# First batch of a scan, attention and expert kernel: x asked for first, u and the projected rows used where they lie, the first time steps two halves at a time, other stores put off

## The chip, the cores and the metric

The kernel runs on one core of a Trainium2 chip. The metric is the device time of one execution in microseconds (us). TensorE is PE in the profile (its weight loads are PEld), VectorE DVE, ScalarE ACT, GpSimd POOL and SyncE SP. SP issues nearly all DMAs of this kernel; its queue entries are SPq.

## What is computed

The input x is (4, 384, 32, 32), four batches of 384 channels on 32 x 32 pixels. Three parts follow each other in each batch; a group normalisation stands before the first.

- A selective scan over four directions (by rows, by columns, and both reversed). For each direction k: `x_dbl = u . x_proj[k]` gives 12 rows for the time step, 16 rows B and 16 rows C; `dt = softplus(dts . dt_proj + bias)`; then for each channel and each of the 16 states, along the 1024 pixels, `h = h * exp(dt * A) + dt * u * B` and `y = sum over the states of h * C`. The four directions' y and `D * u` are added, normalised over the channels, and put through a gelu.
- Windowed causal attention with six heads over 256 tokens, with a gated projection.
- A mixture of four experts, two for each token: 384 to 1536 to 384.

All of it is in f32.

## The kernel before, in words

**Tiles.** Channels lie on the 128 partitions in three tiles (T = 3), pixels along the free dimension (L = 1024, in NH = 2 halves of 512). For the scan a block is 32 channels with 4 states each on the 128 partitions, so a channel tile has 4 blocks (`j`) and a block has 4 groups of states (`g`). A slot is one block and one group, 128 x 1024; there are 16 turns (4 batches x 4 directions) of 48 slots, 768 slots.

**One slot.** `times_b` multiplies dt*u by the B rows into z on POOL, `decay` computes dA = exp(dt * A) on ACT into PSUM, `scan` runs the recurrence on DVE. The product with C follows on POOL (the scan's result then lies in z) or on DVE (it lies in dA), as the planner chooses. `fold_y` adds the 4 states of each channel on PE and adds the sum to what is in DRAM (`ydr`).

**How a slot is fed.** `state_rows` loads B and C rows from DRAM, repeated over 32 channels (`bc`, 512 KB each, 8 for a turn). `time_steps` computes dt and dt*u for one channel tile, in two halves: a matmul of the projected rows `xd` with `dtw` into PSUM (`ps_dt`), then softplus on ACT and DVE, in tiles `ed`; the results go to DRAM (`dtr`), from where `spread` loads them repeated over four states (`dts`).

**Before the first scan.** Constants are loaded on SP's queue; `a4`, the A of every slot, is made from A_logs by four matmuls and a few DVE steps. Then `group_norm(0)`: x is loaded (`xn`) for the moments on DVE, a chain of small matmuls gives mean and scale of each group (`g`), x has meanwhile been loaded again (`un`) and is normalised on ACT, stored as u in `udr`; D * u in two orders is made on ACT (`yd`) and stored to `ydr`. `project` loads u back (`ux`), multiplies it with the projection weights (`ps_x`), copies the result in row order and column order into `xo`, and stores it to `xdr`. `turn_loads` reads the 12 time-step rows back (`xd`) with their weights (`dtw_sb`), `time_steps` reads u once more (`ub`).

**What sets the order.** The whole program is written out ahead of time by a planner (`Machine`). Every generator asks for its next instruction; the planner holds a clock for each engine, costs for each operation, and due times, and picks what can start first, with a bias for EARLY work. So each engine has one fixed order, and another beginning gives another order everywhere. Buffers come from `Stock`s (`wts` of 8 weight tiles, `zs_` of 7 z tiles, `eds` of 3 tiles ed, `pts_` of 3 tiles pt, `banks` of 4 PSUM banks). The first turn's direction is 1, by columns.

The scan of later batches runs while attention and experts of earlier batches fill PE; after the last scan the attention of the last batch and what remains of the experts is left as a tail.

Of the kernel before, what the change touches and what calls it, by code (L numbers as in the profile page):

```python
# [11 lines left out]
F32 = mybir.dt.float32  # L12
# [378 lines left out]
def conv_attn_hybrid(  # L391
# [11 lines left out]
    def const_load(src, shape, name):  # L403
        dst = const.tile(shape, F32, name=name)
        nc.sync.dma_start(dst, src)
        return dst

    xw_sb = const_load(xw, [P, T, KG, XR], "xw_sb")
# [19 lines left out]
    nc.vector.tensor_reduce(dsum, ds_sb.rearrange("p k t -> p t k"), AX.X, ALU.add)  # L428

    fold = const.tile([P, 32], F32, name="fold")  # L430
    nc.vector.tensor_reduce(fold, ident.rearrange("p (d s) -> p d s", s=SG), AX.X, ALU.add)
# [38 lines left out]
    nc.vector.memset(ones, 1.0)  # L470
# [19 lines left out]
    with tc.tile_pool(name="setup", bufs=1) as setup:  # L490
        count_i = setup.tile([P, MB], mybir.dt.int32, name="count_i")
        nc.gpsimd.iota(count_i, pattern=[[1, MB]], base=0, channel_multiplier=0)
        nc.vector.tensor_copy(count, count_i)
        nc.vector.tensor_scalar(count_p, count[:, :SEG], float(P), None, ALU.mult)
        nc.vector.tensor_scalar(base_e, count[:, :NE], float(SEG), None, ALU.mult)
        al_sb = setup.tile([P, KG, T, NS], F32, name="al_sb")
        nc.sync.dma_start(al_sb, alog)
        sel = setup.tile([P, JB, P], F32, name="sel_j")
        nc.gpsimd.memset(sel, 1.0)
        nc.gpsimd.affine_select(  # L500
            sel.rearrange("p j (d s) -> p j d s", s=SG), sel.rearrange("p j (d s) -> p j d s", s=SG),
            pattern=[[-32, JB], [-1, 32], [0, SG]], compare_op=ALU.is_equal, fill=0.0,
            base=0, channel_multiplier=1,
        )
        own = setup.tile([P, SG], F32, name="own")
        nc.vector.tensor_reduce(own, ident.rearrange("p (d s) -> p s d", s=SG), AX.X, ALU.add)
        for j in range(JB):
            ps = banks.now("ps_al")
            pv = ps[:, : KG * T * NS]
            nc.tensor.matmul(  # L510
                pv, sel[:, j, :], al_sb.rearrange("p k t n -> p (k t n)"), start=True, stop=True
            )
            am = setup.tile([P, KG * T * NG, SG], F32, tag="am", name="am")
            nc.vector.tensor_tensor(
                am, pv.rearrange("p (f s) -> p f s", s=SG), bcast(own, KG * T * NG), ALU.mult
            )
            nc.vector.tensor_reduce(
                a4[:, :, :, j, :], am.rearrange("p (k t g) s -> p k t g s", k=KG, t=T), AX.X, ALU.add
            )
            banks.give(ps)  # L520
        m.load_exp_ln()
        m.table = "exp_ln"
        nc.scalar.activation(a4, a4, AF.Exp)
        nc.vector.tensor_scalar(a4, a4, -1.0, None, ALU.mult)

# [14 lines left out]
    pts_ = Stock(m, work, "pt", 3, [P, 4 * P])  # L540
# [4 lines left out]


# [39 lines left out]
    def on_vector():  # L586
        lead = FAVOUR if count_of["scan"] < NSLOT else 0.1
        return m.clock["dve"] + lead < m.clock["act"]

# [48 lines left out]

    def group_norm(b):
# [3 lines left out]
        us_ = us_all if b else zs_  # L643
        mv = rp.tile([P, T, 2], F32, tag="mv", name="mv", bufs=1)

        def moments(t):
            u = yield from us_.take("xn")
            yield from sp.dma_start(u, x[b, ts(t, P)].rearrange("p h w -> p (h w)"))
            st = yield from sts.take("st")
            for h in range(NH):  # L650
                yield from dve.bn_stats(st[:, 6 * h : 6 * h + 6], u[:, ts(h, HB)])
            yield from dve.bn_aggr(mv[:, t, :], st)
            us_.give(u)
            sts.give(st)
# [28 lines left out]
        def normal(t):  # L683
            u = yield from us_.take("un")
            yield from sp.dma_start(u, x[b, ts(t, P)].rearrange("p h w -> p (h w)"))
            yield from act.activation(
                u, u, AF.Identity, bias=g_off[:, t : t + 1], scale=g_rstd[:, t : t + 1]
            )
            yield from sp.dma_start(udr[b][t], u)
            yd = yield from zs_.take("yd")  # L690

# [4 lines left out]
            us_.give(u)  # L696
# [5 lines left out]
            zs_.give(yd)  # L702

        yield from m.together([normal(t) for t in range(T)], T if b == 0 else 1, EARLY)
        have.add(("u", b))


        def project(pair):
            xos = yield from zs_.take("xo", n=2)
            for h in range(NH):  # L710
                us = yield from us_.take("ux", n=2)
                uv = [us[t // NH][:, ts(t % NH, HB)] for t in range(T)]
                for t in range(T):
                    yield from sp.dma_start(uv[t], udr[b][t][:, ts(h, HB)])
# [9 lines left out]
                us_.give(*us)  # L724
                yield from act.copy(xos[0][: 2 * XR, ts(h, HB)], pv)
                yield from copy(
                    xos[1][: 2 * XR, :].rearrange("r (w h) -> r h w", h=HH)[:, ts(h, HH // NH), :],
                    pv.rearrange("r (h w) -> r h w", w=WW),
                )
                banks.give(ps)  # L730
            for n in (1, 0):
                yield from sp.dma_start(xdr[b][2 * pair + n], xos[n][n * XR : (n + 1) * XR, :])
                have.add(("x", b, 2 * pair + n))
            zs_.give(*xos)

        yield from m.together([project(pair) for pair in (0, 1)], 2 if b == 0 else 1, EARLY)

    def turn_loads():
        for i, (b, k) in enumerate(turns):
            yield lambda: ("x", b, k) in have and (i == 0 or (i - 1, T - 1) in dtrs)  # L740
# [7 lines left out]
            xds[i], dtws[i] = xd, dtw_sb  # L748
# [13 lines left out]
    def time_steps():  # L762

        for i, (b, k) in enumerate(turns):
            for t in range(T):
                yield lambda: i in xds and ("u", b) in have and count_of["scan"] >= (i * T + t) * TS - 40
                u = yield from us_all.take("ub")
                yield from sp.dma_start(u, udr[b][t])


                dtr = dram.tile([2, P, L], F32, tag="dtr", name="dtr", bufs=4)
                bias = dtb_sb[:, k, t : t + 1]
                for h in range(NH):
                    c, r = ts(h, HB), slice(32 * h, 32 * h + R)
                    e, dt = yield from eds.take("ed", n=2)
                    w = yield from banks.take("ps_dt", 0)
                    yield from pe.matmul(w, dtws[i][r, ts(t, P)], xds[i][r], start=True, stop=True)
                    yield from act.activation(e, w, AF.Abs, bias=bias)
                    yield from act.activation(dt, w, AF.Relu, bias=bias)
                    yield from act.activation(e, e, AF.Exp, scale=-1.0)  # L780
                    yield from act.activation(w, e, AF.Identity, bias=1.0)
                    yield from dve.scalar_tensor_tensor(e, w, -1.0, e, ALU.add, ALU.subtract)
                    yield from act.activation(w, w, AF.Ln)
                    yield from dve.tensor_tensor(w, w, e, ALU.subtract)
                    yield from dve.tensor_tensor(w, w, dt, ALU.add)
                    if k % 2:
                        v = slice(h * (WW // NH), (h + 1) * (WW // NH))
                        yield from dve.tensor_tensor(
# [807 lines left out]
```

## Time and profile before

| what | value |
|---|---|
| time, median of 4 runs | 3817.52 us (3815.51 to 3819.78) |
| profiled execution, its own time | 3820.98 us |
| its span | 3819.2 us |
| busy share: PE, DVE, ACT, POOL | 79%, 77%, 58%, 74% |
| mean granted clock of PE | 0.83 |
| first scan starts | 97.90 us |
| last scan ends | 3117.97 us |
| DMA over the span | 953.64 MB, 250 GB/s |

The span is the profiled time from the first to the last instruction. A share is a mean over stages with different limits, so what matters is when each engine is busy: the lines are shown with the prediction. In the order of time a row gives start, length, engine, operation, result and inputs, and in brackets the idle time of the engine before it with what ended it. Buffer numbers are left out of names. A helper records nearly all operations, so most have its lines, L148 or L159; rows are told apart by their tiles. A matmul in f32 leaves two records.

### The profile page before, as it was taken

What the parts mean: (1) busy time and instruction counts of PE and PEld (TensorE: products, weight loads), DVE (VectorE), ACT (ScalarE), POOL (GpSimd) and SP (SyncE); (2) the same over time, 40 slices, a digit from 0 to 9 for tenths busy, and PEclk for the clock granted to TensorE, in tenths of its full rate; (3) what the DMA queues carried; (4) which work ended last, traced back from release to release, by engine and by line L of the source; (5) the groups of instructions that cost most, each with busy time, mean ns of one, the idle gap of its engine ahead of it and who ended that gap; (6) DMA issues with size and microseconds to landing.
All of it is one profiled execution on the core that took longest, in us unless ns stands there. A gap on an engine that the chain in (4) does not pass through costs nothing. (4 is left out here: it accounts for less than half of the span.)

```text
span 3819.2 us, 50289 instructions
## 1 busy us (share of the span) xinstructions
PE 3006.0 (79%) x15892; PEld 1822.5 (48%) x15892; DVE 2932.8 (77%) x3341; ACT 2220.9 (58%) x4028; POOL 2810.7 (74%) x1469
## 2 busy tenths in 40 slices
PE   2555545578797899877678788898898999998998
PEld 1100010035564555544356445565555668777886
DVE  2999999998889999999988989988789963321001
ACT  2545545467676677776667576777767654442221
POOL 0999998999888887999988699898889960102001
PEclk8555556578798899986779899998898999998997
DMA  5776775444468899944478789675679974468995
GB/s 198 270 263 219 266 261 216 169 161 142 162 226 344 324 370 324 365 159 159 137 251 281 281 321 345 241 252 179 219 266 362 348 258 149 159 212 306 318 318 189
DMA packets 394144, 953.64 MB, mean 250 GB/s; under 512 B 49620, under 2 KB 173400, under 8 KB 393880
## 3 DMA queue, kind: packets, MB, share of 16 engines
q1 hardware_dynamic: 385688, 925.27, 68.5%
q0 software_dynamic: 8192, 25.17, 1.9%
q8 instruction: 126, 2.06, 0.2%
q14 instruction: 138, 1.13, 0.1%
HBM read 786.39 MB, written 182.78 MB: 254 GB/s over the span
## 5 line engine op out<-in xcount | busy, mean ns | idle before, releaser
L148 POOL TENSOR_TENSOR z<-dts,bc 128x1024 f32<-128x1024 f32 x768 | 1792.5, 2360 | 124.3 <-DMA dts<-dtr 65.0
L148 ACT ACTIVATE dA<-dts,a 128x1024 f32<-128x1024 f32 x768 | 855.3, 1118 | 531.3 <-DVE z L148 509.8
L159 PE MATMUL ps_y<-z,fold 128*32 128x512 f32 x3072 | 719.5, 763 | 421.9 <-POOL z L148 234.8
L148 DVE TENSOR_TENSOR_SCAN dA<-dA,z 128x1024 f32<-128x1024 f32 x414 | 946.6, 2286 | 73.3 <-ACT dA L148 53.4
L148 POOL TENSOR_TENSOR z<-z,bc 128x1024 f32<-128x1024 f32 x354 | 830.0, 2357 | 100.2 <-DVE z L148 97.0
L148 DVE TENSOR_TENSOR_SCAN z<-dA,z 128x1024 f32<-128x1024 f32 x354 | 797.0, 2275 | 19.1 <-ACT dA L148 15.0
L159 PEld LDWEIGHTS ps_hid<-xbt,w_sb 128*128 128x128 f32 x5472 | 663.1, 197 | 138.3 <-issue 41.6
L159 PE MATMUL y_ff<-w_sb,hs 128*128 128x384 f32 x1824 | 686.5, 517 | 35.3 <-ACT hs L159 30.9
L159 PE MATMUL ps_hid<-xbt,w_sb 128*128 128x128 f32 x5472 | 687.5, 282 | 25.4 <-ACT xbt L148 9.7
L148 DVE TENSOR_TENSOR z<-dA,bc 128x1024 f32<-128x1024 f32 x414 | 505.2, 1220 | 14.5
L159 PEld LDWEIGHTS ps_y<-z,fold 128*32 128x32 f32 x3072 | 93.6, 120 | 847.1 <-POOL z L148 419.9
L148 ACT ACTIVATE hs<-ps_hid,bb 128x128 f32<-128x128 f32 x912 | 273.4, 364 | 384.1 <-PE ps_hid L159 318.6
L159 PEld LDWEIGHTS y_ff<-w_sb,hs 128*128 128x128 f32 x1824 | 342.6, 201 | 282.7 <-issue 60.5
L148 POOL DMA_INDIRECT cb<-ysdr,idx x64 | 62.4, 975 | 321.1 <-DMA ysdr<-yb 270.7
L159 POOL TENSOR_TENSOR rn<-rn,half 128x1 f32<-128x1 f32 x96 | 52.8, 550 | 233.0 <-DVE rn L159 201.4
L148 DVE COPY yb<-y_ff 128x384 f32<-128x384 f32 x22 | 12.3, 558 | 270.5 <-PE y_ff L159 209.0
L148 POOL DMA_INDIRECT xsdr<-tks,idx x64 | 65.1, 1017 | 178.8 <-DMA xsdr<-tks,idx 67.8
L148 PE MATMUL ps_dt<-xd,dtw_sb 12*128 12x512 f32 x192 | 141.3, 836 | 23.2 <-DMA dtw_sb<-in_dtw_dram 15.3
L148 ACT ACTIVATE ed<-ps_dt,dtb_sb 128x512 f32<-128x512 f32 x192 | 123.8, 680 | 44.4 <-PE ps_dt L148 33.6
L148 DVE TENSOR_TENSOR ps_dt<-ps_dt,ed 128x512 f32<-128x512 f32 x192 | 132.5, 690 | 10.4 <-ACT ps_dt L148 7.8
L148 ACT COPY ed<-ps_dt 128x512 f32<-128x512 f32 x96 | 56.0, 584 | 130.2 <-DVE ed L148 130.0
L159 PEld LDWEIGHTS ps_o<-v,pt 128*128 128x128 f32 (+1 forms) x720 | 93.8, 206 | 16.6 <-ACT pt L148 3.7
(204 smaller groups left out, 3380.8 us busy)
## 6 DMA issues: line engine op xcount, KB each, us to landing
w_sb<-wl SPq DMA_DIRECT2D x608, 576.0 KB
dts<-dtr SPq DMA_DIRECT2D x384, 512.0 KB
bc<-xdr SPq DMA_DIRECT2D x128, 512.0 KB
dtr<-ed SPq DMA_DIRECT2D x192, 256.0 KB
ub<-udr SPq DMA_DIRECT2D x48, 512.0 KB
yp<-ydr SPq DMA_DIRECT2D x96, 256.0 KB
ydr<-yp SPq DMA_DIRECT2D x96, 256.0 KB
wl<-in_w_dram SPq DMA_DIRECT2D x32, 576.0 KB
```

The source lines that it names most:

```text
L148: return getattr(self.real, op)(*a, **k)
L159: getattr(self.real, op)(*a, **k)
```

## The change

- Constants are loaded on ACT's queue in place of SP's, A_logs and the projection weights first, the weights in two loads with the two directions of a pair swapped; x is what SP asks for first.
- `a4`, `dsum`, `fold` and the counts are no longer made ahead of everything; a generator `constants` makes them after the first batch's normalisation.
- First batch only: x stays in three tiles of `wts` and is normalised there; `project`, `time_steps` read u there. x is not loaded again, u is not read back.
- First batch only: the projection makes the pair with the first turn's direction first, the second pair waits until the first z product has been issued. The first turn's time steps read the projected rows in `xo`.
- `half_step` is one half of a channel tile's time steps; in the first turn both halves are in work together, with six `ed` tiles (three of them lent by `pts_`), in later turns one after the other as before.
- First batch only: storing u, and making and storing D * u (`keep`), wait until z products have been issued. `fold_y` waits for them, `decay` for `a4`.

```diff
     def const_load(src, shape, name):
-        nc.sync.dma_start(dst, src)
+        nc.scalar.dma_start(dst, src)
...
-    xw_sb = const_load(xw, [P, T, KG, XR], "xw_sb")
+    al_sb = const_load(alog, [P, KG, T, NS], "al_sb")
+    xw_sb = const.tile([P, T, KG, XR], F32, name="xw_sb")
+    for n in range(2):
+        nc.scalar.dma_start(xw_sb[:, :, 1 - n :: 2, :], xw[:, :, n::2, :])
...
-    pts_ = Stock(m, work, "pt", 3, [P, 4 * P])
+    pts_ = Stock(m, work, "pt", 0, [P, 4 * P])
+    eds.add(work, "pt", 3, [P, 4 * P])
...
+    def constants():
+        yield lambda: "normal" in have
+        yield from dve.tensor_reduce(dsum, ds_sb.rearrange("p k t -> p t k"), AX.X, ALU.add)
+        have.add("dsum")
...
+        for j in range(JB):
...
+            ps = yield from banks.take("ps_al")
+            yield from pe.matmul(pv, sel_j[:, j, :], al_sb.rearrange("p k t n -> p (k t n)"), start=True, stop=True)
...
+        yield from act.activation(a4, a4, AF.Exp)
+        yield from dve.tensor_scalar(a4, a4, -1.0, None, ALU.mult)
+        have.add("a4")
...
     def group_norm(b):
-        us_ = us_all if b else zs_
+        us_ = us_all if b else wts
...
         def normal(t):
-            u = yield from us_.take("un")
-            yield from sp.dma_start(u, x[b, ts(t, P)].rearrange("p h w -> p (h w)"))
+            if b:
+                ut = yield from us_.take("un")
+                yield from sp.dma_start(ut, x[b, ts(t, P)].rearrange("p h w -> p (h w)"))
+            else:
+                ut = first_u[t]
+            u = ut[:, :L]
             yield from act.activation(
                 u, u, AF.Identity, bias=g_off[:, t : t + 1], scale=g_rstd[:, t : t + 1]
             )
+            if b:
+                yield from keep(t, ut)
+                us_.give(ut)
+
+        def keep(t, ut):
+            u = ut[:, :L]
+            if not b:
+                yield lambda: count_of["times"] > t and "dsum" in have
             yield from sp.dma_start(udr[b][t], u)
...
         def project(pair):
-            xos = yield from zs_.take("xo", n=2)
+            if not b and pair:
+                yield lambda: count_of["times"] > 0
+            xos = yield from (zs_ if b else wts).take("xo", n=2)
...
+                else:
+                    uv = [first_u[t][:, ts(h, HB)] for t in range(T)]
...
+            if not b and pair == 0:
+                xds[0] = [xos[1][:R, ts(h, HB)] for h in range(NH)]
...
     def time_steps():
-                u = yield from us_all.take("ub")
-                yield from sp.dma_start(u, udr[b][t])
+                if i:
+                    u = yield from us_all.take("ub")
+                    yield from sp.dma_start(u, udr[b][t])
+                else:
+                    u = first_u[t][:, :L]
...
+                halves_ = [half_step(i, t, h, u, dtr) for h in range(NH)]
+                yield from m.together(halves_, 1 if i else NH, EARLY)
...
     def decay():
-            yield lambda: (n, 0) in spreads
+            yield lambda: (n, 0) in spreads and "a4" in have
...
     def fold_y(n):
+        yield lambda: ("yd", b, t) in have and "fold" in have
```

## The prediction

> **What bounds the kernel now.** I read the head of the page and its 40 slices first, to see which engine is full when.
>
> ```profile
> span 3819.2 us, 50289 instructions
> PE 3006.0 (79%) x15892; PEld 1822.5 (48%) x15892; DVE 2932.8 (77%) x3341; ACT 2220.9 (58%) x4028; POOL 2810.7 (74%) x1469
> DVE  2999999998889999999988989988789963321001
> POOL 0999998999888887999988699898889960102001
> ```
>
> A slice is 95.5 us. DVE and POOL are almost empty in the first one, full until about slice 33, almost empty after it. So there are three stages, and I cut the busy time by stage, at the start of the first scan and the end of the last (columns: length, then busy time and count of PE, PEld, DVE, ACT, POOL, then clock and DMA).
>
> ```profile
> 0.00:97.90 97.90, 26.27 (x64) 11.56 (x64) 25.17 (x52) 25.00 (x31) 11.63 (x25) 0.82 0.58 202
> 97.90:3117.97 3020.07, 2329.25 (x11759) 1282.30 (x11760) 2777.41 (x2813) 1975.03 (x3357) 2732.72 (x1348) 0.80 0.71 254
> 3117.97:3819.20 701.23, 650.52 (x4070) 528.65 (x4068) 130.25 (x476) 220.87 (x641) 66.31 (x97) 0.94 0.70 237
> ```
>
> The scan stage is bound by DVE and POOL together (92% and 90% busy), the tail by PE (93%). In the first stage no engine is busy over 27%: it is one chain of waits, and the whole program hangs behind it. The change works there, so I read that stage in order of time (start, length, engine, operation; in brackets what ended the idle time).
>
> ```profile
> 13.46 1.28 SPq L148 DMA_DIRECT2D xn<-in_x_dram  x3
> 16.92 1.29 DVE L148 BATCH_NORM_STATS2 st<-xn 128x6 f32<-128x512 f32 x2 [2.91 <-DMA xn<-in_x_dram]
> ...
> 28.50 2.37 ACT L148 ACTIVATE un<-un,g 128x1024 f32<-128x1024 f32 x2 [14.79 <-DVE g L148]
> ...
> 39.95 14.63 SPq L148 DMA_DIRECT2D ux<-udr  x12
> ...
> 44.25 7.81 PE L159 MATMUL ps_x<-ux,xw_sb 128*88 128x512 f32 x12 [17.20 <-DMA ux<-udr]
> ...
> 59.52 1.27 SPq L148 DMA_DIRECT2D bc<-xdr  x2
> ...
> 68.70 0.31 SPq L148 DMA_DIRECT2D dtw_sb<-in_dtw_dram  x1
> ...
> 75.81 3.75 PE L148 MATMUL ps_dt<-xd,dtw_sb 12*128 12x512 f32 x6 [7.40 <-DMA dtw_sb<-in_dtw_dram]
> ...
> 76.86 1.02 DVE L148 TENSOR_TENSOR ed<-ps_dt,ub 128x512 f32<-128x512 f32 x1 [3.19 <-DMA ub<-udr]
> ...
> 87.70 6.25 SPq L148 DMA_DIRECT2D dts<-dtr  x8
> ...
> 92.44 2.35 POOL L148 TENSOR_TENSOR z<-dts,bc 128x1024 f32<-128x1024 f32 x1 [64.21 <-DMA dts<-dtr]
> ...
> 96.68 1.12 ACT L148 ACTIVATE dA<-dts,a 128x1024 f32<-128x1024 f32 x1 [2.66 <-DMA dts<-dtr]
> 97.90 2.30 DVE L148 TENSOR_TENSOR_SCAN dA<-dA,z 128x1024 f32<-128x1024 f32 x1 [4.50 <-POOL z L148]
> ```
>
> The reader sees x asked for only at 13.46, behind the constants; u written out and read back (28.50 to 44.25); and a weight of 18 KB asked for at 68.70 that comes at 75.8, because it lies in the DMA queue behind 4 MB of state rows (bc), as u (ub) does.
>
> **The change, step by step (the new start of the scan).**
> 1. x first. Issued at 0.80 in place of 13.46; the first statistics came 3.46 later, so about 4.3. But the third x load now waits on a semaphore that it shares with the load of A_logs; ds_sb took 2.07 from issue to use, so it is issued near 2.9 and lands between 6.4 (2.9 + 3.46) and 7.9 (the third before was used at 19.97, 6.5 after the first issue, which with small loads beside it I put at 7.1 after). I take 7.9. From there 1.63 to the gather of means (19.97 to 21.60) and 6.90 to ACT's first normalisation (21.60 to 28.50): 16.4. The constants moved to ACT's queue are all issued before that; the reductions for a4, dsum and fold now fall to DVE while it waits for PE.
> 2. u where it lies. One normalisation (1.19), then PE: 17.6, in place of 44.25. The 15.75 us of writing u, its ydr copies and reading it back are gone from the path.
> 3. Projection, one pair of scan directions only. Six matmul records of the first half took 5.25 (44.25 to 49.50, 0.86 each), the next six ran at 0.43 each; with one ps_al of 0.73 between: 5.25 + 0.73 + 2.6 = 8.6, then DVE's copy 1.02: 27.3. If PE stays at 0.86 it is 29.9.
> 4. State rows. The store of xdr to its first reader took 2.0 (57.19 to 59.19), so bc is issued at 29.3. From the first bc issue to the arrival of the weight queued behind it was 16.3 (59.52 to 75.81): the queue is clear at 45.6.
> 5. Time steps, two halves at once. From xo in SBUF: PE, then ACT's abs, relu, exp, identity, ln (0.69, 0.58, 0.63, 0.60, 0.58) and DVE's 0.69, twice 0.72 and 1.02 for both halves interleaved; ACT's eleven steps up to the second ln sum to 6.5 with the a4 exp of 0.36, DVE adds 4.5 after them (0.72 three times, 0.2, 1.02 twice), PE 1.1 before: the second half's product is ready at 39.4, against 8.8 more for the second half before (76.86 to 85.67). But its store lies behind bc: with four stores of 256 KB at about 0.7 each (380 GB/s in this stretch) the third lands at 47.6. So the doubled chunks win little by themselves, and bc sets the time. If the stores do not queue behind bc, it is 43.
> 6. dts to the first scan. 87.70 to 97.90 was 10.2; in the new order of SP the decay's dts is fourth, not third, in the queue: 512 KB, 1.3 more. First scan 47.6 + 11.5 = **59.1**, bounds 54.5 (step 5) and 63 (steps 3 and 6 late). That is **38.8 us earlier**.
>
> **What is put off.** Three udr stores, twelve ydr stores, three yd activations on ACT (1.95 each) and the second pair's projection (two DVE copies of 1.02, one after the first scan) come beside the first scans. ACT is 65% busy in that stage; DMA 71%. SP waits at the first ydr store for yd, which stands on ACT behind four decays, until about 67.6; behind it stands the dts of the fifth block, issued near 71, landed near 76. POOL needs it as its 25th operation, 22 products of 2.36 and some small ones after 52.3, near 107. Cover 31 us, so I cost it nothing; without that cover every us late is a us lost. Half a time step (2.9 on DVE) moves ahead of the first scan.
>
> **The scan stage.** The planner writes out another order for everything. These rows price the counts that changed:
>
> ```profile
> L148 POOL TENSOR_TENSOR z<-z,bc 128x1024 f32<-128x1024 f32 x354 | 830.0, 2357 | 100.2 <-DVE z L148 97.0
> L148 DVE TENSOR_TENSOR z<-dA,bc 128x1024 f32<-128x1024 f32 x414 | 505.2, 1220 | 14.5
> L159 PE MATMUL y_ff<-w_sb,hs 128*128 128x384 f32 x1824 | 686.5, 517 | 35.3 <-ACT hs L159 30.9
> L159 PE MATMUL ps_hid<-xbt,w_sb 128*128 128x128 f32 x5472 | 687.5, 282 | 25.4 <-ACT xbt L148 9.7
> ```
>
> Five products with C go from DVE to POOL: 5 x 2.357 = 11.8 more on POOL; on DVE 5 x 1.22 = 6.1 less, 2.9 less from step 5, 1.0 more for xo, some 2 more for copies: 6 less. Both engines feed each other, so I take the mean, **+2.9**. Bounds: a tenth of DVE's 243 us of idle time in this stage either way, 24, for what an order can win or lose.
>
> **The tail.** After the last fold PE now has 9 more ps_hid and 3 more y_ff matmuls, one expert's chunk that no longer fits under the scan. 687.5 / 2736 = 0.251 and 686.5 / 912 = 0.753 per matmul (two records each): 2.3 + 2.3 = **+4.5**.
>
> **Sum.** The profiled execution took 3820.98 (1.78 around its span): 3820.98 - 38.8 + 2.9 + 4.5 = 3789.6. The median of the four runs, 3817.52, is 3.46 lower, so I forecast 3786.
>
> **Two rules against rows.** In step 3 PE's records took 0.86 for 5.25 us and then 0.43, while the granted clock read 1.00 all the time from 44 to 52 us; I go by the records. "TensorE: Matmul & The Clock Gate" of the Trainium skill (What's actually happening) says that a cold array runs at half rate until about 3.4 us of busy time; by that the first half would cost 3.4 + 0.9 = 4.3, an estimate, and the sum be 1 us less. Against the change speaks "DMA: Bandwidth & Descriptors" (Issuing engines are not separate DMA queues; Specifications): loads from another engine's queue run on the same 16 DMA engines and save only issue time, and pieces under 512 bytes miss line rate. The projection weights now come in pieces of 176 bytes (44 floats), beside x. No row here prices such a load; if it held x up by its own share, step 1 would be later by a few us, as an estimate, and the sum with it.
>
> **Rivals.**
> - Given back: the start comes early, but the new order idles DVE and POOL for 24 to 39 us more, 10 to 16% of DVE's idle time. For: POOL has 12 us more and is 90% full. Against: 409 and 359 scans in place of 414 and 354, nearly the same plan. Time 3810 to 3825. Chance 0.07.
> - Slower: SP's order. If the put-off stores hold the dts of block five past 107 (step above), POOL, then DVE, stand still. To end above 3825 the loss must be 39 us: dts issued near 141 and not 71, with SP 70 us at yd. Against: yd waits for four decays only. Time 3830 to 3850. Chance 0.05.
> - The early start doubly good: stores not behind bc (54.5) and an order that idles less by a tenth: 3786 - 4.6 - 24 = 3757, or lower. Chance 0.08.
> - Forecast: start near 59, the rest as before: 3758 to 3809. Chance 0.80.
>
> The range takes the forecast's bounds: 3757 to 3810. About 0.2%, 7.6 us, is what a measurement of this kernel tells from no change. Faster 0.88 (forecast and the doubly good), same 0.07, slower 0.05.
>
> **What would show it.** Right: in the new timeline first statistics at 4 to 5, ACT's normalisation at 15 to 17, bc at 28 to 31, dts at 46 to 49, first scan at 56 to 62, then DVE and POOL at 92 to 98 of 96 us as after 97.9 now, a scan stage of 3010 to 3035, a tail of 700 to 710. Step 5 is wrong if the dtr stores land before bc. Wrong as a whole: a POOL wait of tens of us for dts between 80 and 200, or a scan stage longer by over 30.

## The result, and the profile after

The changed kernel takes 3814.44 us (median of 52 runs, 3798.48 to 3827.73), the kernel before 3820.78 in the runs beside it (78 runs, 3806.47 to 3836.79). The ratio is 0.9983, with a 95% interval of 0.9977 to 0.9990: 6 us faster, where 31 were forecast (3786 against 3817.52). The profiled execution took 3807.42 us, its span is 3805.5.

The busy time by stage, cut again at the first scan's start and the last scan's end (length, then busy time and count of PE, PEld, DVE, ACT, POOL, clock, DMA share and GB/s):

```profile
0.00:56.82 56.82, 29.19 (x66) 12.29 (x66) 23.77 (x54) 20.38 (x32) 13.11 (x26) 0.83 0.55 190
56.82:3100.40 3043.58, 2336.17 (x11734) 1288.54 (x11735) 2780.30 (x2812) 1984.25 (x3350) 2747.70 (x1354) 0.80 0.71 253
3100.40:3805.50 705.10, 653.96 (x4099) 533.87 (x4098) 131.38 (x477) 221.31 (x645) 64.02 (x96) 0.95 0.70 237
```

The start is 41.1 us shorter (97.90 to 56.82), the tail 3.9 longer (701.23 to 705.10). The scan stage has grown from 3020.07 to 3043.58, by 23.5, with DVE only 2.9 and POOL 15.0 busier. One trace is one execution, and the times of these 52 runs spread over 29 us, so a stage's length read from one trace can be off by some 10 us, as an estimate. The start in order of time, with the rows that answer to those shown of before:

```profile
0.80 4.42 SPq L148 DMA_DIRECT2D xn<-in_x_dram  x3
...
4.72 1.29 DVE L148 BATCH_NORM_STATS2 st<-xn 128x6 f32<-128x512 f32 x2 [3.76 <-DMA xn<-in_x_dram]
...
17.49 3.50 ACT L148 ACTIVATE xn<-xn,g 128x1024 f32<-128x1024 f32 x3 [5.39 <-DVE g L148]
...
18.78 5.40 PE L159 MATMUL ps_x<-xn,xw_sb 128*88 128x512 f32 x6 [2.70 <-ACT xn L148]
...
24.34 2.74 PE L159 MATMUL ps_x<-xn,xw_sb 128*88 128x512 f32 x6
...
30.85 5.25 SPq L148 DMA_DIRECT2D bc<-xdr  x8
...
38.35 1.91 SPq L148 DMA_DIRECT2D dtr<-ed  x4
...
45.39 1.28 ACT L148 ACTIVATE ed<-ps_dt,dtb_sb 128x512 f32<-128x512 f32 x2 [3.20 <-DMA dtr<-ed]
...
46.63 5.73 SPq L148 DMA_DIRECT2D dts<-dtr  x8
...
50.29 2.35 POOL L148 TENSOR_TENSOR z<-dts,bc 128x1024 f32<-128x1024 f32 x1 [33.04 <-DMA dts<-dtr]
...
56.82 2.30 DVE L148 TENSOR_TENSOR_SCAN dA<-dA,z 128x1024 f32<-128x1024 f32 x1 [2.83 <-ACT dA L148]
```

The reader sees x asked for at 0.80, no writing and reading back of u, and one long gap left: the dtr stores are issued at 38.35, but the first step that waits for one of them to be done (ACT, for its ed tile) starts at 45.39, and the dts loads that read them are issued at 46.63, because the stores lie in the DMA queue behind the 4 MB of bc issued from 30.85 on.

From here on scans and slots are counted from 0, so that the 48th has 48 ahead of it. By the start of a scan the lead over the kernel before is 41.1 us at the first, 37.0 at the 48th, 39.4 at the 192nd, 49.5 at the 288th, 12.3 at the 480th, 36.0 at the 672nd and 17.6 at the last. So little of it is given back near the change. Most is lost more than 1000 us behind it (the 288th scan starts at 1137 us).

### The profile page after: what moved, and what is told of

The parts are those of the page before. It is cut to its first block, busy times and chain, and to the rows that moved or that the text cites. A ratio compares the mean times of both kernels' runs of the same rounds, so it can differ in the third digit from the quotient of the medians.

```text
span 3805.5 us, 50230 instructions
## 1 busy us (share of the span) xinstructions
PE 3019.3 (79%) x15898; PEld 1834.7 (48%) x15898; DVE 2935.4 (77%) x3343; ACT 2225.9 (58%) x4024; POOL 2824.8 (74%) x1475
## 5 line engine op out<-in xcount | busy, mean ns | idle before, releaser
L148 POOL TENSOR_TENSOR z<-dts,bc 128x1024 f32<-128x1024 f32 x768 | 1793.5, 2364 | 129.1 <-PE ps_y L159 66.2
L148 DVE TENSOR_TENSOR_SCAN dA<-dA,z 128x1024 f32<-128x1024 f32 x409 | 935.2, 2287 | 79.0 <-ACT dA L148 55.2
L148 POOL TENSOR_TENSOR z<-z,bc 128x1024 f32<-128x1024 f32 x359 | 842.5, 2361 | 111.8 <-DVE z L148 96.4
L148 DVE TENSOR_TENSOR_SCAN z<-dA,z 128x1024 f32<-128x1024 f32 x359 | 808.0, 2276 | 34.0 <-ACT dA L148 32.5
L159 PE MATMUL ps_hid<-xbt,w_sb 128*128 128x128 f32 x5472 | 697.6, 285 | 49.8 <-DMA w_sb<-wl 14.1
L159 PE MATMUL y_ff<-w_sb,hs 128*128 128x384 f32 x1824 | 677.6, 513 | 39.2 <-ACT hs L159 31.3
L148 PE MATMUL ps_dt<-xd,dtw_sb 12*128 12x512 f32 x180 | 125.4, 794 | 14.8 <-ACT yl L148 8.0
L148 ACT COPY ed<-ps_dt 128x512 f32<-128x512 f32 x96 | 56.2, 586 | 103.3 <-DVE ed L148 103.0
L159 PEld LDWEIGHTS ps_o<-v,pt 128*128 128x128 f32 (+1 forms) x720 | 104.9, 227 | 16.6 <-DVE k L148 2.8
```

The lines of the kernel that those rows point to most:

```text
L148: return getattr(self.real, op)(*a, **k)
L159: getattr(self.real, op)(*a, **k)
```

## The experiments

**Is it the order?** The planner's order of one version (which instruction next, and which engine takes a product) was written down, and a kernel made that begins as one version does and from the 48th scan on follows the order of the other. A kernel that follows its own order this way keeps it: in the traces of the changed kernel and of top_in_psum_new_order (below), every engine's instructions stand in the same order, the edited ones included. The core of the edit:

```diff
-            for e, c in self.pending.items():
-                if c:
-                    t0, p = self.choose(e)
...
+            follow = self.plan and self.switch()
+            if follow:
+                every = [(self.plan[0].get(p[2].key, -1), n, p) for n, p in enumerate(p for c in self.pending.values() for p in c)]
+                if every:
+                    p = min(every, key=lambda q: q[:2])[2]
...
+        m.plan, m.switch = plan_of(PLAN), lambda: count_of["scan"] >= SWITCH
```

*new_start_old_order*: the changed kernel's start, the order of before from the 48th scan on.

> The changed kernel's beginning up to the 48th scan, and from there each engine's instructions in the order that the kernel before has. Theory (the gain of the start is real, and the planner's other order of the scan stage gave it back): first scan near 56.8 us, a lead of about 37 us over the kernel before at the 49th scan that is kept to the end, time 3775 to 3790 us. Rival (the early start itself, or the work put off behind it, costs later by contention or clock, in any order): time stays near 3814 us, the lead melts between the 400th and the 500th scan as in the changed kernel.

Measured 3784.28 us (4 runs, 3781.42 to 3792.24), ratio 0.9912 [0.9878, 0.9945]; first scan at 56.0, scan stage 3025, tail 699.4. The start is as good as in the changed kernel, a lead of 37.0 us is still there at the last scan, and the time is the one that the prediction gave for the change (3786).

*old_start_new_order*: the reverse.

> The beginning of the kernel before up to the 48th scan, and from there the order of the changed kernel. Theory (order): first scan at 97.9 us, scan stage about 24 us longer than before, tail about 4 us longer, time 3843 to 3856 us. Rival (early start itself): time as before, 3821 us.

Measured 3856.26 us (4 runs, 3853.01 to 3865.31), ratio 1.0091 [1.0059, 1.0123]; first scan at 95.8, scan stage 3055.9, tail 711.9: the time is at the upper end of the forecast, the stage 36 us longer and the tail 11, where 24 and 4 were expected. The order costs with either start, 27 us with the new one (0.9983 against 0.9912) and 35 with the old. It does so in the same places: the 48 slots from the 672nd are 19.7 us longer in the new order with the new start and 18.6 with the old one; from the 288th it is 16.8 and 14.8, from the 384th 14.1 and 16.5, and from the 576th both get some back, 10.8 and 13.8.

*new_start_lead65* and *old_start_lead65*: one number by which the planner gives products to POOL, changed from the 48th scan on. Each start gets another order from it.

```diff
-            on_pool = ... and m.clock["pool"] < m.clock["dve"] + LEAD
+            on_pool = ... and m.clock["pool"] < m.clock["dve"] + (LEAD if s < SLOT_0 else 0.65)
```

> The changed kernel with one number of the planner other from the 48th scan on: POOL gets the product with C when its clock is less than 0.65, not 0.60, ahead of DVE's. Nothing of the start changes. Theory (orders differ by luck): first scan near 56.8 us, but the time differs from 3814 us by 10 to 40 us in either direction, the tail 30 to 50 us longer (99 more first-layer and 33 more second-layer matmuls of the experts after the last fold, 25 us each) and the scan stage shorter or longer. Rival (the order hardly matters): 3814 us within 8.

Measured 3835.39 us (10 runs, 3829.98 to 3847.45), ratio 1.0039 [1.0024, 1.0054]; scan stage 3052.5, tail 729.8. The tail is 25 us longer than the changed kernel's, not 30 to 50.

> The kernel before with the same one number, 0.65 from the 48th scan on. Theory (orders differ by luck): another time than 3821 us by 10 to 40 us in either direction, with first scan at 97.9 us; the tail has 54 fewer first-layer and 15 fewer second-layer matmuls, 25 us less. Rival (order hardly matters): 3821 us within 8.

Measured 3829.36 us (10 runs, 3819.27 to 3839.72), ratio 1.0015 [0.9995, 1.0034]; scan stage 3057.6, tail 683.0. The time hardly moved, less than the 10 to 40 us expected: in the traced execution, the slowest of the ten, 37 us more in the scan stage and 18 less in the tail stand against each other. One number, with no part of the computation changed, moves the scan stage by nearly the whole gain of the start here; with the new start it moved it by 9.

**What is each part of the change worth?** All four have the changed kernel's start but for one edit, and the order of before from the 48th scan on, so the 3784 (0.9912) above is their foot. The intervals of all four overlap with the foot's: the times don't tell the parts apart, the starts in the traces do.

*part_one_half*:

```diff
-                    yield from m.together(halves_, NH, EARLY)
+                    yield from m.together(halves_, 1, EARLY)
```

> New start, old order from the 48th scan on, but the first turn's time steps one half at a time, as before. Theory (the state rows in the DMA queue set when the first time steps land, as the prediction's step 5 says): second half ready near 45.5 us instead of 39.3, dts issued near 48 instead of 46.6, first scan near 57.5 instead of 56.0, time 3784 to 3788 us. Rival (the two halves at once are worth what they take less in ACT and DVE): first scan 62 to 64 us, time 3790 to 3793 us.

Measured 3781.29 us (3774.25 to 3785.46), ratio 0.9891 [0.9864, 0.9917]; dts issued at 46.91 (46.28 in the foot), first scan at 56.2 (56.0). Two halves at once are worth 0.2 us of the start here: the stores wait for bc either way.

*part_x_last*:

```diff
-        nc.scalar.dma_start(dst, src)
+        nc.sync.dma_start(dst, src)
...
-        nc.scalar.dma_start(xw_sb[:, :, 1 - n :: 2, :], xw[:, :, n::2, :])
+        nc.sync.dma_start(xw_sb[:, :, 1 - n :: 2, :], xw[:, :, n::2, :])
```

> New start, old order from the 48th scan on, but the constants on SP's queue ahead of x. Theory: 14 issues of 0.47 put x's load to 7.4 us, everything behind it moves by 6.6 us: first scan 62.6 us, time 3789 to 3793 us. Rival (x first is covered by the chain behind it): first scan 56 us, time 3784 us.

Measured 3790.56 us (3779.00 to 3794.48), ratio 0.9924 [0.9899, 0.9950]; x is asked for at 8.08, the first scan starts at 62.2. x first is worth 6 us of the start.

*part_stores_first*:

```diff
-                yield lambda: count_of["times"] > t and "dsum" in have
+                yield lambda: "dsum" in have
...
-        yield from m.together([project(pair) for pair in (0, 1)], 1, EARLY)
         if b == 0:
-            yield from m.together([keep(t, first_u[t]) for t in range(T)], 1, EARLY)
+            yield from m.together([keep(t, first_u[t]) for t in range(T)], T, EARLY)
             have.add(("u", b))
+        yield from m.together([project(pair) for pair in (0, 1)], 1, EARLY)
+        if b == 0:
```

> New start, old order from the 48th scan on, but u stored and D*u made and stored ahead of the projection, not put off. Theory: three activations of 1.95 on ACT beside PE's first matmuls and 3 MB at about 380 GB/s, 8 us, in the DMA queue ahead of the projected rows' store and the state rows: first scan 62 to 67 us, time 3788 to 3795 us. Rival (stores are covered): first scan 56 us, time 3784 us.

Measured 3778.01 us (3774.66 to 3785.99), ratio 0.9894 [0.9866, 0.9921]. The time is below the expected 3788 to 3795. The first scan starts at 59.7, 3.7 later than in the foot but earlier than the 62 to 67 expected, and the 48th at 225.8 where the foot has 227.6: what the stores cost ahead of the scan, the put-off stores cost behind its start.

*plus_rows_late*: the first turn's bc in parts, behind the loads and stores that the first scan needs.

```diff
                 yield lambda: ("x", b, k) in have
+                if i == 0 and g == 1:
+                    yield lambda: (0, 0) in dtrs
+                if i == 0 and g > 1:
+                    yield lambda: all((n, q) in spreads for n in (0, 1) for q in (0, 1))
```

> New start, old order from the 48th scan on, and the first turn's state rows held back: the first group's two as before, the second group's behind the stores of the first time steps, the third's and fourth's behind the first four dts. Theory (the state rows in the queue set the start): the stores land near 42.5 us instead of 46.6, first scan 50 to 53 us instead of 56.0, time 3778 to 3781 us. Rival (not the queue, or POOL then waits for the rows): first scan 55 us or later, or a wait of POOL for bc that takes it back, time 3784 us.

Measured 3780.31 us (3770.07 to 3782.44), ratio 0.9896 [0.9872, 0.9920]. In its start the bc loads come in four parts:

```profile
30.08 1.27 SPq L165 DMA_DIRECT2D bc<-xdr  x2
39.58 1.17 SPq L165 DMA_DIRECT2D bc<-xdr  x2
41.00 4.52 SPq L165 DMA_DIRECT2D dts<-dtr  x7
...
46.50 6.96 POOL L165 TENSOR_TENSOR z<-dts,bc 128x1024 f32<-128x1024 f32 x3 [29.13 <-DMA dts<-dtr]
...
50.24 2.30 DVE L165 TENSOR_TENSOR_SCAN dA<-dA,z 128x1024 f32<-128x1024 f32 x1 [1.27 <-ACT dA L165]
```

dts is issued 5.3 us sooner than in the foot, the first scan starts 5.8 sooner, and 5.2 of it are still there at the 48th. So bc in the queue did set the start.

**What in the order costs?** The first suspicion came from this row and its idle time in the changed kernel (busy time, mean ns, idle time before, with what ended it). POOL waits 66.2 us for a z tile to be read by the fold on PE; in the kernel before the same wait came to 36.5 (second row: total, times, longest).

```profile
L148 POOL TENSOR_TENSOR z<-dts,bc 128x1024 f32<-128x1024 f32 x768 | 1793.5, 2364 | 129.1 <-PE ps_y L159 66.2
```

```profile
POOL z L148 <- PE ps_y L159: 36.5, 22, 5.8
```

To try it, an eighth z tile was added to both orders. It needs room, so in all four runs of this group one of two xbt tiles and one of two yp tiles were taken away.

```diff
-TILES, EPS, NZ = 3, 1e-5, 7
+TILES, EPS, NZ = 3, 1e-5, 8
...
-        Stock(m, work, tag, n, [P, D]) for tag, n in (("xb", 1), ("xbt", 2), ("hs", NHS), ("yb", 1))
+        Stock(m, work, tag, n, [P, D]) for tag, n in (("xb", 1), ("xbt", 1), ("hs", NHS), ("yb", 1))
-    yps = Stock(m, work, "yp", 2, [P, LH])
+    yps = Stock(m, work, "yp", 1, [P, LH])
```

*small_7z_new_order* and *small_7z_old_order* (without the first line of the edit):

> The changed kernel's own recorded order from the 48th scan on, with one xbt tile in place of two and one yp tile in place of two (both of the experts and of the gelu), to make room for the run beside it; 7 z tiles as before. Both theories expect about the changed kernel's time, 3814, up to 15 more for the tiles taken away. It is the foot that the 8 z tiles are compared with.

Measured 3881.02 us (3875.75 to 3888.38), ratio 1.0153 [1.0131, 1.0175].

> The same start and the same tiles taken away, with the order of the kernel before from the 48th scan on. Both theories expect it 25 to 35 below the run in the new order with 7 z tiles, as the two orders stood apart with all tiles.

Measured 3866.10 us (3858.74 to 3874.69), ratio 1.0105 [1.0080, 1.0130]. Both miss: the two tiles cost 65 and 74 us by the ratios, not up to 15, and the orders are 15 apart, not 25 to 35. Why so much is open, and with a foot that far off these runs say little of the kernel with all its tiles.

*big_8z_new_order* and *big_8z_old_order*:

> As the run with 7 z tiles in the new order, with an eighth z tile. Theory that the new order loses its time because z tiles come free late (POOL waits at z for the fold's matmul on PE, 66 us in place of 36): the eighth tile takes most of these waits away, POOL z <- PE ps_y falls below 20, and the time falls by 20 to 30, to about that of the old order. Rival, the new order loses it elsewhere (by where steps of ACT and DVE stand between decays and scans), and the waits at z only show it: the time falls by less than 10, and the wait on PE turns into waits on ACT and DVE.

Measured 3864.41 us (3860.35 to 3882.96), ratio 1.0123 [1.0093, 1.0153].

> As the run with 7 z tiles in the old order, with an eighth z tile. Theory of the z tiles: little left to win, 0 to 12 less, and the two orders then lie within 10 of each other. Rival: the two orders stay 20 to 35 apart with 8 z tiles as with 7.

Measured 3877.00 us (3874.50 to 3878.72), ratio 1.0140 [1.0123, 1.0158]. POOL's waits in the new order (engine, tile, what it waited for; total, times, longest), first with 7 z tiles, then with 8:

```profile
POOL z L165 <- DVE z L165: 116.6, 54, 12.6
POOL z L165 <- PE ps_y L176: 109.9, 47, 12.2
```

```profile
POOL z L165 <- DVE z L165: 165.1, 67, 12.6
POOL z L165 <- PE ps_y L176: 41.3, 14, 9.5
```

The wait for the folds falls by 69 us, the wait for DVE rises by 49, and the time falls by 17 (by the ratios 11, with intervals that touch). In the old order the eighth tile makes the kernel slower by 11, so that the two orders do come within 13 us of each other (7 by the ratios), the new one now ahead, but half of that is the old order's loss. The theory of the z tiles is not borne out, nor is its rival's "less than 10". A kernel further down settles more: no_two_inputs_new_order is 35 us faster than the changed kernel with this wait as long as before:

```profile
POOL z L165 <- PE ps_y L176: 69.4, 36, 6.3
```

So a gain of more than the 27 us that the order lost was to be had with the wait for the folds left as it is. Whether that wait has a part in the loss is not shown.

**A step on DVE that should take 0.2 us.** Comparing the 48 slots from the 672nd in the changed kernel and in new_start_old_order, window by window (columns as above), showed that DVE itself was 11.8 us busier:

```profile
2725.20:2937.60 212.40, 174.31 (x1004) 114.68 (x1003) 192.11 (x225) 137.87 (x261) 186.86 (x97) 0.90 0.74 256
```

```profile
2726.30:2919.00 192.70, 169.33 (x982) 107.41 (x981) 180.29 (x203) 137.41 (x248) 178.02 (x89) 0.92 0.90 320
```

In that window of the changed kernel, in order of time, DVE and then POOL:

```profile
2864.02 0.17 DVE L159 TENSOR_REDUCE r<-p 128x4 f32<-128x16 f32 x1
2864.66 13.15 DVE L159 TENSOR_TENSOR ps_r<-p,r 128x16 f32<-128x16 f32 x1 [0.47 <-DVE r L159]
```

```profile
2861.61 4.66 POOL L148 TENSOR_TENSOR z<-z,bc 128x1024 f32<-128x1024 f32 x2
2866.24 11.53 POOL L148 TENSOR_TENSOR z<-dts,bc 128x1024 f32<-128x1024 f32 x5
2890.37 2.35 POOL L148 TENSOR_TENSOR z<-z,bc 128x1024 f32<-128x1024 f32 x1 [12.61 <-DVE z L148]
```

A subtraction of 16 elements on each partition, in the router of the experts, is on record as 13.15 us of busy DVE. It begins while POOL runs a product and ends at 2877.81, when POOL's row of products without a gap ends (2866.24 + 11.53 = 2877.77). Then POOL has to wait 12.61 us for DVE. I call such a time a stall: a step of DVE that takes over 0.5 us more than the shortest of its kind. Over the whole kernel the eight instructions of this kind are (shortest, median, longest in ns):

```profile
L159 DVE TENSOR_TENSOR ps_r<-p,r x8: 184/820/13146, 951.2 to 3379.3; 128x16 f32<-128x16 f32 x8
```

The old order has its own: in new_start_old_order a copy of means (g<-mv, 128x3) takes 9.32 us and ends at 1245.09, as POOL's row does at 1245.05.

```profile
1235.77 9.32 DVE L165 COPY g<-mv 128x3 f32<-128x3 f32 x1
```

```profile
1238.12 6.93 POOL L165 TENSOR_TENSOR z<-dts,bc 128x1024 f32<-128x1024 f32 x3
```

The kernel before had it too, 10.02 us long, up to the end of POOL's row (1275.07 + 6.92 = 1281.99):

```profile
1272.00 10.02 DVE L148 COPY g<-mv 128x3 f32<-128x3 f32 x1
```

```profile
1275.07 6.92 POOL L148 TENSOR_TENSOR z<-dts,bc 128x1024 f32<-128x1024 f32 x3
```

Most stalls are short, though, and end with the product that POOL then runs, while POOL goes straight on to the next. So it is with another of the eight subtractions of the changed kernel:

```profile
951.19 1.80 DVE L159 TENSOR_TENSOR ps_r<-p,r 128x16 f32<-128x16 f32 x1
```

```profile
950.61 2.35 POOL L148 TENSOR_TENSOR z<-dts,bc 128x1024 f32<-128x1024 f32 x1
952.92 2.34 POOL L148 TENSOR_TENSOR z<-z,bc 128x1024 f32<-128x1024 f32 x1
```

In the scan stages of all twenty traces of this case, 31 stalls lasted longer than one of POOL's products, 2.65 to 13.5 us, and every one of them ended where POOL paused (0.16 us or more). Of the 212 others, none over 2.41 us, 149 ended with POOL going straight on. What decides whether a step gets in at the first end of a product or has to wait for a pause, no run here shows.

"SBUF — State Buffer" of the Trainium skill (Who interferes with whom) says which steps these are: DVE and GpSimd share a pair of SBUF ports as an exclusive lock, and a DVE instruction with two SBUF inputs, or a copy or cast in a 2-port mode, contends for it. (SBUF and PSUM are the two memories on the core in which this kernel's tiles lie.) Scans and most products of this kernel read one operand from PSUM. The traces agree on that: all 243 stalls are steps with two operands from SBUF, the copy g<-mv, or a cast (idx<-place). But the page gives the lock to the first comer for one instruction. The short stalls agree with that too; in the long one here a waiting DVE step sat through the rest of one POOL instruction and five more.

I summed the stalls of each trace's scan stage, and then made runs in which these steps read only one operand from SBUF.

*top_in_psum_new_order* (the changed kernel's own order) and *top_in_psum_old_order*:

```diff
+        top = part(PT)
-        mm.tensor_reduce(r, p, AX.X, ALU.max)
-        mm.tensor_tensor(pp, p, bcast_last(r, NE), ALU.subtract)
+        mm.tensor_reduce(top, p, AX.X, ALU.max)
+        mm.tensor_tensor(pp, p, bcast_last(top, NE), ALU.subtract)
```

> The changed kernel's own order, unchanged from the first instruction to the last; only the row maximum that the router subtracts lies in PSUM in place of SBUF, so that the 128x16 subtraction reads one operand from SBUF in place of two (8 such subtractions). Theory that this instruction cannot run while POOL's products follow each other without a gap, and that this is the loss: it takes under 0.3 us in all 8 places, the 48 slots from the 672nd take 195 to 200 in place of 212, and the time falls by 12 to 20 from the changed kernel's, to 3794 to 3803. Rival, the stall only shows a wait that DVE would have had anyway (for z or dA): the instruction gets short, another wait takes its place, and the time falls by less than 4. Second rival, where the operand lies has nothing to do with it: the instruction still takes 13 us.

Measured 3802.20 us (6 runs, 3796.19 to 3810.30), ratio 0.9940 [0.9922, 0.9959]: 12 less by the medians, 16 by the ratios. The subtraction is now one of 56 steps of its tiles, none of which takes over 0.18 us:

```profile
L176 DVE TENSOR_TENSOR ps_r<-p,ps_r x56: 166/171/180, 951.4 to 3380.5; 128x12 f32<-128x12 f32 x16, 128x4 f32<-128x4 f32 x16, 128x8 f32<-128x8 f32 x16, 128x16 f32<-128x16 f32 x8
```

The 48 slots got only 8 us shorter, to 204, not 195 to 200: a later step there, the comparison with count_p, now takes 5.0 in place of 2.3.

> The same operand in PSUM with the changed kernel's start and the order of the kernel before from the 48th scan on, in which the 8 subtractions took 0.2 to 2.3 us, 7.7 above their shortest in all. Theory: 0 to 6 less than without it (3784), most likely 3; the two orders then lie 10 to 18 apart in place of 30. Rival: no less, and the orders as far apart as before.

Measured 3779.49 us (6 runs, 3774.02 to 3784.47), ratio 0.9882 [0.9864, 0.9900]: 5 less by the medians, 11 by the ratios, whose intervals overlap. The two orders are still 23 us apart, by the ratios 22, not 10 to 18: on that the forecast missed.

*few_two_inputs_new_order*: also these.

```diff
-        yield from dve.tensor_copy(mean, mv[:, :, 0])
+        yield from dve.tensor_reduce(mean, mv[:, :, :1], AX.X, ALU.max)
...
+        g_mean, off = ps[:, 8 : 8 + T], ps[:, 16 : 16 + T]
...
-                yield from dve.tensor_tensor(dev, dev, dev, ALU.mult)
-                yield from dve.tensor_tensor(dev, dev, mv[:, :, 1], ALU.add)
+                yield from dve.tensor_tensor(off, dev, dev, ALU.mult)
+                yield from dve.tensor_tensor(dev, off, mv[:, :, 1], ALU.add)
...
-            mm.tensor_tensor(total, cn[:, PT, :], total, ALU.add)
+            mm.tensor_tensor(cum, cn[:, PT, :], total, ALU.add)
...
-            mm.tensor_tensor(full, bcast_last(total, SEG), bcast(count_p, NE), ALU.is_gt)
+            mm.tensor_tensor(full, bcast_last(cum, SEG), bcast(count_p, NE), ALU.is_gt)
...
```

> As the first of these, and also the copy of the means, the steps to the scale and the router's comparison with count_p read at most one operand from SBUF or are made by a reduction; one product of 128x3 still reads two. In the changed kernel these took 25 us above their shortest in all, none of them over 3.5. Theory: 0 to 12 less than with the row maximum alone, most likely 5, since short stalls are partly covered. Rival: no less.

Measured 3784.26 us (6 runs, 3773.00 to 3795.41), ratio 0.9893 [0.9872, 0.9914]: 18 less again, more than expected. The one step left with two operands from SBUF took the place of the others:

```profile
457.60 8.32 DVE L165 TENSOR_TENSOR ps_gm<-g 128x3 f32<-128x3 f32 x1
```

*no_two_inputs_new_order*: that one too.

```diff
...
-                yield from dve.tensor_tensor(dev, mean, g_mean, ALU.subtract)
-                yield from dve.tensor_tensor(off, dev, dev, ALU.mult)
+                yield from dve.tensor_tensor(off, mean, g_mean, ALU.subtract)
+                yield from dve.tensor_tensor(dev, mean, g_mean, ALU.subtract)
+                yield from dve.tensor_tensor(off, off, dev, ALU.mult)
...
```

> As the run in the new order in which few of the small steps on DVE read two operands from SBUF, with the last of them, the square of the group norm's differences, changed too: one operand now lies in PSUM. Theory that each such stall holds DVE back for its length: 8.3 and 4.3 us go, and the time falls by 4 to 12 from 3784, to 3772 to 3780. Rival, a stall of some us ahead of a group norm is covered, since DVE waits there for PE anyway: no change within 4.

Measured 3779.22 us (6 runs, 3775.09 to 3789.93), ratio 0.9881 [0.9857, 0.9906]: 5 less, within the intervals, so this last step alone is not told from no change. DVE's busy time in the scan stage is now 2734.77, 45.5 us below the changed kernel's, as much as the stalls there had come to; POOL's is the same within 3.

*plus_all* joins the old order, bc late, stores not put off and the operands of few_two_inputs; *plus_all_no_two_inputs* has the last step as well.

> The changed kernel's start with the state rows of the first turn held back and the stores not put off, the old order from the 48th scan on, and all of these operands in PSUM. In the old order a copy of means (128x3) took 9.3 us and the others 22 above their shortest. Theory: the first scan at 52 to 56, and 6 to 18 less than the run with the state rows held back alone (3780): 3762 to 3774. Rival, nothing from the operands: 3776 to 3782.

Measured 3771.72 us (5 runs, 3760.82 to 3778.09), ratio 0.9864 [0.9845, 0.9884]; first scan at 54.2.

> The same step changed in the run that joins what has won. Theory: a stall of 6.3 us goes, 2 to 7 less than 3772, so 3765 to 3770. Rival: no change within 3.

Measured 3767.16 us (5 runs, 3756.59 to 3768.47), ratio 0.9847 [0.9822, 0.9872], 5 less, within the intervals here too. It is the fastest of all, by the ratio 58 us below the kernel before.

The stalls and the times side by side (stalls over 0.5 us in the scan stage, from one trace each):

| kernel | order | stalls | their sum, us | ratio |
|---|---|---|---|---|
| before | old | 15 | 37.2 | 1 |
| the changed kernel | new | 16 | 44.6 | 0.9983 |
| top_in_psum_new_order | new | 12 | 27.7 | 0.9940 |
| few_two_inputs_new_order | new | 2 | 12.3 | 0.9893 |
| no_two_inputs_new_order | new | 0 | 0 | 0.9881 |
| new_start_old_order | old | 15 | 32.4 | 0.9912 |
| top_in_psum_old_order | old | 10 | 24.7 | 0.9882 |
| plus_rows_late | old | 14 | 31.4 | 0.9896 |
| plus_all | old | 4 | 9.3 | 0.9864 |
| plus_all_no_two_inputs | old | 1 | 0.7 | 0.9847 |
| new_start_lead65 | lead 0.65 | 19 | 39.5 | 1.0039 |

In the new order 44.6 us of stalls were worth 0.0102 of the time, 39 us (29 to 49 by the intervals), nearly as much as they lasted. In the old one 31 were worth less: 0.0049 or 19 us from plus_rows_late to plus_all_no_two_inputs, of which the stores not put off may be up to 0.0018 (0.9894 against 0.9912 in part_stores_first, inside the intervals), so 12 to 19 us.

How much of the 27 us between the two orders goes with the stalls is open. By these figures it is 20 or more; if the old order is reckoned from top_in_psum_old_order, with the 24.7 us of stalls left there at the same worth (10 to 15 us), it is 12 to 17. Each ratio has an interval of some 10 us either way, and no run has the changed kernel's start and the old order with these operands changed and nothing else. Place by place, the new order without stalls has won back most of the 48 slots from the 672nd (212.4 to 198.5, the old order has 192.7) and half of the difference from the 288th (205.0 to 197.1, against 188.2), but nothing from the 384th: 193.6 to 195.8, against 179.5. There the new order puts more of the other work, 942 matmul records in the changed kernel where the old order has 744. Nor are stalls all that lead 0.65 costs: the scan stage of new_start_lead65 is 28 us longer than that of new_start_old_order, with 7 us more of them. What the rest of its loss is, no run here tells.

## Why the prediction failed, step by step

| step | forecast | measured in the changed kernel |
|---|---|---|
| 1 first statistics, third x used, first normalisation | 4.3, 7.9, 16.4 | 4.72, 8.94, 17.49 |
| 2 PE starts on the projection | 17.6 | 18.78 |
| 3 copy to xo ended | 27.3 | 28.13 |
| 4 bc issued | 29.3 | 30.85 |
| 5 second half's product | 39.4 | 39.26 |
| 5 third store landed, dts issued | 47.6 | 46.63 |
| 6 first scan | 59.1 | 56.82 |
| put-off work | 0 | 4 by the 48th scan |
| scan stage | +2.9, bounds 24 either way | +23.5 |
| DVE's, POOL's busy time in it | -6, +11.8 | +2.9, +15.0 |
| tail | +4.5 | +3.9 |

Steps 1 to 4 run 0.4 to 1.6 us late, mostly from the third x load, which was issued at 4.90 and not near 2.9; step 5 lands 1.0 early, dts to first scan took 10.2 and not 11.5. So the first scan comes 2.3 earlier than forecast, with errors of both signs in the sum. Step 5's choice, that the bc loads and not the halves set the time, was right, and the runs showed both sides of it: one half at a time costs 0.2 us of the start, bc held back wins 5.8. Put-off work did cost: the lead falls from 41.1 to 37.0 by the 48th scan, and part_stores_first shows that putting it off wins nothing by then. The pages weighed in the prediction: the first six projection records took 5.40 us, as the rows of before had it (5.25), and not the estimate of 4.3 worked out from "TensorE: Matmul & The Clock Gate" (What's actually happening); and x, beside which the weights now come in pieces under the 512 bytes of "DMA: Bandwidth & Descriptors" (Specifications), took 3.92 from issue to first use in place of 3.46, half a microsecond and not a few.

**The step that failed is "The scan stage", +2.9.** It was priced by counts: five products from DVE to POOL, copies and half steps, at their mean durations. The counts came out as said (409 and 359 products with C), and POOL's busy time rose by 15.0, near the 11.8 priced. DVE's was to fall by 6 and rose by 2.9; that this is the very +2.9 given for the stage is chance. Of the 9 us between, 7.4 are stalls (44.6 where the kernel before had 37.2). The stage grew by 23.5 in the profile, and by about 31 if the profile's start and tail are held against the medians (41.1 - 3.9 - 6.3). What the runs showed in its place: the same start with the old order takes 3784, so it is the other fixed order that costs, 27 us. The rival "Given back" had the right stage and time (3810 to 3825), at 0.07, and the right reason, the other order, though in the profile DVE idles 20.6 and POOL 8.5 us more and not 24 to 39 both. What in that order costs is shown in part: stalls, and something that is open.

Why 0.07 was too low can be read from the profile of before, and was not. I took DVE's 2777 busy microseconds for work, and looked for what an order can lose in its 243 idle ones alone. 37 of the busy ones were small steps standing still while POOL multiplied, one of them for 10.0 us. How long such a step stands depends on what the order has put beside it on POOL (the longest is 13.15 us in the new order, 9.3 in the old one, 5.7 in new_start_lead65), so this term changes with the order, and the engine behind can wait as long again: in the new order the step of 13 us was followed by a POOL wait of 12.6. My bound of a tenth of the idle time had no row behind it; lead 0.65 moves the stage by 37 us with the old start, in one trace.

## What to carry to other kernels

A change at the start of a program whose order is written ahead is two changes: the start, and another order for all that follows. Price the second by what two orders of the same work differ by, and test a start under a fixed order. And before taking an engine's busy time for work, list the longest of each kind of small step beside the shortest: here a group with a shortest of 184 ns and a longest of 13146 cost 12 to 16 us, a third of what the start had won, and one operand moved to PSUM won that back.

## What the hardware showed that I had not expected

- A DVE step with two operands from SBUF, or the copy of means, begun while POOL multiplies, stood until a product of POOL ended, and where it was not let in at the first end it stood until POOL paused: 13.15 us through the rest of one product and five more, 9.32 and 8.32 us in other orders, each ending within 0.1 us of POOL's row. All 31 stalls over 2.45 us ended at a pause; 149 of the 212 shorter ones did not. Taking one of these steps away let a later one stand longer (2.3 to 5.0, 2.3 to 8.32).
- 512 KB loads that are already in the queue hold up a 256 KB store issued 7.5 us behind them: 7.0 us from the issue of the four dtr stores (38.35) to the first step that needs one done (45.39). With three of four pairs of bc held back, dts went out 5.3 us sooner.
